# Preparation of a four-layer graph network on one core: adjacency casts issued earlier, the first head's scores by a product, x loaded by rows

## The chip, the cores and the metric

The kernel runs on one core of a Trainium2 chip, in one launch. The metric is the device time of an execution in microseconds (us). The kernel before took 2358.74 us (median of three runs, 2350.66 to 2361.85). The profile is one further execution of 2364.72 us, whose span from the first to the last instruction is 2363.0 us.

## The reference

Four layers in a row work on the same 4096 nodes with 64 features and a dense 4096 x 4096 adjacency of zeros and ones. Each is `x = x + layer(relu(layernorm(x)))`. The change lies in layer 0, a graph attention with eight heads of 32 features, six on the features and two whose scores come from given "intent" vectors:

```python
mask = (adj > 0)[None]
Wh_s = jnp.einsum('nf,hfo->hno', x, W_sp)
f1 = jnp.einsum('hno,ho->hn', Wh_s, a_sp[:, :NHID])
f2 = jnp.einsum('hno,ho->hn', Wh_s, a_sp[:, NHID:])
e_s = jax.nn.leaky_relu(f1[:, :, None] + f2[:, None, :], ALPHA)
h_s = jax.nn.elu(_masked_attend(e_s, mask, Wh_s))     # softmax over the neighbours, times Wh_s
... # two intent heads alike, their scores from intent_embeds
Who = h @ W_out
... # one more attention over Who, its scores from a_out
```

Layers 1 to 3 (a hyperbolic layer, a mean over neighbours, and one that weights the last 100 neighbours) are not touched.

## The kernel before, in words

The 4096 nodes are 32 blocks of 128 (`NB` = 32, `P` = 128). Since exp(leaky_relu(a + b)) is a product of two factors on each side of a + b = 0, a head's softmax sums need only the sign of a + b for each pair of nodes. For a head and a half of the receiving nodes (2048 of them, `HW`) the kernel does, for each pair of sender blocks `j0`:

- two signs `st`, 128 x 2048 each, from `srow` (the receivers' scores, the same row on all 128 partitions) and the senders' scores `nt`: on ScalarE, every fifth one on VectorE (`split_edges`, L1127 and L1132);
- `B`, the signs and the adjacency bits `mres`, and for most pairs `C`, the remaining edges (VectorE, L1136 and L1140);
- the sums `accB`, `accD`, `accC`, `accL` on TensorE (L1371), with the head's values `ybh` and `ych` as weights.

Such a head and half is called a unit here; there are sixteen, half 0 first. In unit 0 TensorE also forms `dm`, the sums that tell of receivers without edges, with `YD` as weights and the raw `mres` as data. At a unit's end ScalarE copies accB (L1506) and accC, VectorE accD and accL.

**The adjacency.** `mres` is eight buffers, each four sender blocks by 2048 receivers, one byte an entry. GpSimd's queue loads them from the float32 adjacency and casts on the way, 4 MB read for 1 MB written each. Four are issued in the preparation (L1160), the other four when `srow` of unit 0 has landed (`transfers_after`, L1090 to L1093, makes GpSimd read one element first). The other half of the receivers is cast later in the same manner, in the units of heads 1 to 4.

**The preparation.** Two 512 KB loads bring `x` with nodes `(b p)`: block b, partition p. SyncE's queue then loads `FT`'s intent rows, the weights `rh` (W_sp, W_int and four vectors of a_int) and `ab` (a_sp). GpSimd loads `rho` (W_out) and `abo` (a_out). `layernorm_relu` (L943 to L953) makes `h` in two halves; `feature_rows` transposes it (`tr`, L959) and copies it to `FT` (L960); `w2sq`, `Mh`, `Qh` scale the weights; `pa` makes the score columns; `pw` (L1010) the output's score columns in `rho`. Then TensorE forms `pst` (all scores by node and head 0's values `z0`, L1236) and `prs` (scores as rows, L1260). The rows go to memory (`srow_d`, L1269) and come back on all partitions (`srow`, L1328). Exponentials `wn`, `fz` and the splits `fd`, `YD`, `ybh`, `ych` follow (`value_steps`, L1185 to L1191, L1104 to L1113). `mean` and `meanq` are the values of receivers without edges.

The values of the other seven heads are formed inside unit 0, in eight groups k (L1453): four products `pwh`, two copies into parts of `h` and `x`, which are free by then, and a store to `Z_d`. Each unit of half 0 reads its next head's part back (`zt`).

A scheduler sets the order on each engine from the order in the source and from what an instruction depends on[...]. Pools give memory: a pool opened after another has closed takes its place, and its first users wait for the last users of what lay there before. The signs `st`, `B`, `C` of the units lie in the pool `hwork`, opened after the preparation's pools have closed:

```python
B, C = split_edges(
    work,                       # pool "hwork"
    srow,
    nt[:, j0 : j0 + 2, hd],
    edges,
```

Of the kernel before, what the change touches and what calls it, by code (L numbers as in the profile page):

```python
# [9 lines left out]
F32 = mybir.dt.float32  # L10
BF16 = mybir.dt.bfloat16
F16 = mybir.dt.float16
# [6 lines left out]
ALU = mybir.AluOpType  # L19
AX = mybir.AxisListType  # L20
# [4 lines left out]
P = 128  # L25
N = 4096
NB = N // P
D = 64
# [802 lines left out]
def kernel(  # L831
# [67 lines left out]

    def load_x():  # L900
        for bs in halves:
            nc.sync.dma_start(x[:, bs], x_in.rearrange("(b p) f -> p b f", p=P)[:, bs])

    load_x()
    h = npool.tile([P, NB, D], F32, name="h")

# [29 lines left out]

    def layernorm_relu():
        with tc.tile_pool(name="ln", bufs=1) as wide:
            for bs in halves:
                nb = bs.stop - bs.start  # L940
                hb = h[:, bs]
                mean = small("ln_mean", nb)
                nc.vector.tensor_reduce(mean, x[:, bs], AX.X, ALU.add)  # L943
                nc.vector.tensor_scalar(mean, mean, 1.0 / D, None, ALU.mult)
                nc.vector.tensor_tensor(hb, x[:, bs], over(mean, D), ALU.subtract)
                sq = wide.tile([P, nb, D], F32, name="ln_sq", tag="wide")
                nc.vector.tensor_tensor(sq, hb, hb, ALU.mult)
                var = small("ln_var", nb)
                nc.vector.tensor_reduce(var, sq, AX.X, ALU.add)
                nc.scalar.activation(var, var, AF.Sqrt, bias=eps_t, scale=1.0 / D)  # L950
                nc.vector.reciprocal(var, var)
                nc.vector.tensor_tensor(hb, hb, over(var, D), ALU.mult)
                nc.vector.tensor_scalar(hb, hb, 0.0, None, ALU.max)  # L953
# [43 lines left out]
    with ExitStack() as l0:  # L997
# [4 lines left out]
        rho = lp.tile([P, NC2, D + 2], F32, name="rho")  # L1002
        nc.gpsimd.dma_start(rho[:, :, 0:D], W_out.rearrange("(c p) o -> p c o", p=P))
        abo = lp.tile([P, 2, D], F32, name="abo")
        nc.gpsimd.dma_start(
            abo.rearrange("p s d -> p (s d)"), a_out.unsqueeze(0).to_broadcast([P, 2 * D])
        )
        for s in range(2):
            pw = spool.tile([P, NC2, D], F32, name="pw", tag="pw")
            nc.vector.tensor_tensor(  # L1010
                pw,
                rho[:, :, 0:D],
                abo[:, s : s + 1, :].to_broadcast([P, NC2, D]),
                ALU.mult,
            )
            nc.vector.tensor_reduce(rho[:, :, D + s], pw, AX.X, ALU.add)

        def feature_loads(hp):
# [15 lines left out]
            for i in range(HI):  # L1034
# [7 lines left out]
                a_sp.rearrange("h o -> (h o)").unsqueeze(0).to_broadcast([F, HS * 2 * O]),  # L1042
            )
            return FT, rh, ab

# [11 lines left out]

        def feature_rows(FT, ps):
            for g in range(NG):
                transpose_to(  # L1060
                    FT[0:F, g * G : (g + 1) * G],
                    [h[:, b, :] for b in range(g * GB, (g + 1) * GB)],
                    F,
                    ps,
                    nc.scalar.copy,
                )
# [14 lines left out]
        def edges_of(q, hf):  # L1081
            return adjT[q * JT * P : (q + 1) * JT * P, hf * HW : (hf + 1) * HW].rearrange(
                "(t p) i -> p t i", p=P
            )
# [10 lines left out]
        def first_half(q):  # L1095
            return mres[q].bitcast(F8), edges_of(q, 0)


# [3 lines left out]
        def split16(hi, lo, src, tmp):  # L1102

            nc.scalar.copy(hi, src)  # L1104
            nc.vector.tensor_tensor(tmp, src, hi, ALU.subtract)
            nc.scalar.activation(lo, tmp, AF.Copy, scale=LO)  # L1106
# [47 lines left out]
        YD = lp.tile([P, NB, 4, NH], BF16, name="YD")  # L1154
        nc.gpsimd.memset(YD, 0.0)
        Mh = lp.tile([P, NH], F32, name="Mh")
        meanq = lp.tile([P, NH, 2, O], F16, name="meanq")
        nc.gpsimd.memset(meanq, 0.0)
        for q in range(NQ // 2):
            nc.gpsimd.dma_start(*first_half(q))  # L1160
        srow_d = dram.tile([NH, N], F32, name="srow_d")
# [5 lines left out]
        Z_d = dram.tile([NB // 4, P, (NH - 1) * 4 * O], F32, name="Z_d")  # L1167
        vpool = ea.enter_context(tc.tile_pool(name="values", bufs=2))

        def value_tiles():  # L1170
# [28 lines left out]
        with ExitStack() as pa:  # L1199
# [28 lines left out]
            nc.vector.tensor_copy(rhz[0:F, 2 * NH :], rhq[:, 0:O])  # L1228
            layernorm_relu()
            feature_rows(FT, ps)  # L1230
            st16 = hp.tile([P, NB, 2 * NH], F32, name="st16")
            z0 = hp.tile([P, NB, O], F32, name="z0")
            for b0 in range(0, NB, 8):
# [14 lines left out]
            cm = col_maxs(tm, NH, "cmax")  # L1248
            
            cm = cm.unsqueeze(1).to_broadcast([P, NB, NH])  # L1250

            rs = hp.tile([K0, O], F32, name="rs")
            nc.vector.memset(rs, 0.0)
            nc.vector.tensor_copy(rs[:, 0:NH], rh[:, HO : HO + NH])
            sr = hp.tile([P, 2, G], F32, name="sr")
            for k in range(2):
# [38 lines left out]
            pss = ps.tile([P, HO], F32, name="pss", tag="misc")  # L1295
            nc.tensor.matmul(pss, lhsT=frep, rhs=rhq, start=True, stop=True)
            mean = work.tile([P, NH, O], F32, name="mean", bufs=1)
            nc.scalar.copy(mean, pss.rearrange("p (h o) -> p h o", o=O))
            mhl = work.tile([P, NH, 2, O], F16, name="mhl", bufs=1)
            split16(mhl[:, :, 0, :], mhl[:, :, 1, :], mean, mean)  # L1300
            for q in range(NS):
                nc.scalar.copy(meanq[q * O : q * O + 1], mhl[q * O : q * O + 1])
        with ExitStack() as ha:
# [4 lines left out]

            by_g = h.rearrange("p b d -> p (b d)").rearrange("p (s i) -> p s i", i=G)
            def load_products(zt, hd):  # L1310
                src = Z_d.rearrange("k p (h i) -> p k h i", h=NH - 1)[:, :, hd - 1, :]
                nc.sync.dma_start(zt.rearrange("p (k b) o -> p k (b o)", b=4), src)

            pending = None
            for hf in range(2):
# [9 lines left out]
                for hd in range(NH):  # L1325
                    first = hd == 0
                    srow = vpool.tile([P, HW], F32, name="srow", tag="srow")
                    nc.sync.dma_start(  # L1328
                        srow,
                        srow_d[hd : hd + 1, hf * HW : (hf + 1) * HW].to_broadcast([P, HW]),  # L1330
                    )
                    if hf == 0 and first:
                        transfers_after(srow[0:1, 0:1], *(first_half(q) for q in range(NQ // 2, NQ)))
                    yb, yc = now
# [46 lines left out]
                    for j0 in range(0, NB, 2):  # L1381
# [4 lines left out]
                        B, C = split_edges(  # L1386
                            work,
                            srow,
# [52 lines left out]
                        if hf == 0 and hd > 0 and j0 % (NB // 2) == 8 and later:  # L1441
                            transfers_after(B.bitcast(U8)[0:1, 0, 0:4], *later.pop(0))
                        if hf == 0 and first and j0 < NB // 2:

                            k = j0 // 2
                            Z = (h, x)[k // 2 % 2].rearrange("p b d -> p (b d)").rearrange(
                                "p (s i) -> p s i", s=2
                            )[:, k % 2, 0 : (NH - 1) * 4 * O]
                            for b in range(0, 4, 2):
                                pw = ps.tile([P, 2, NH - 1, O], F32, name="pwh", tag="misc")  # L1450
                                for i in range(2):
                                    c = (4 * k + b + i) * P
                                    nc.tensor.matmul(  # L1453
                                        pw[:, i].rearrange("p h o -> p (h o)"),
                                        lhsT=FT[0:F, c : c + P],
                                        rhs=rhq[:, O:],
                                        start=True,
                                        stop=True,
                                    )
                                (nc.vector.tensor_copy if b else nc.scalar.copy)(  # L1460
                                    Z.rearrange("p (h b o) -> p b h o", b=4, o=O)[:, b : b + 2], pw
                                )
                            nc.sync.dma_start(Z_d[k], Z)
                        if hf == 0 and first and j0 == NB // 2 + 2:
                            load_products(zt, hd + 1)
                        if j0 >= (NB // 2 + 6 if first else NB // 2 - 2):
                            next(coming, None)
# [1054 lines left out]
```

## Time and profile before

| | us |
|---|---|
| Median of three runs (lowest, highest) | 2358.74 (2350.66, 2361.85) |
| Profiled execution | 2364.72 |
| Its span | 2363.0 |
| TensorE busy over the span | 1990.4 (84%) |
| VectorE busy | 1842.6 (78%) |
| ScalarE busy | 1666.3 (71%) |
| GpSimd busy | 82.9 (4%) |
| First accB product of unit 0 | 77.44 |
| Copy of accB, units 0 and 1 | 148.74, 211.02 |

A row of the timeline names the start, the busy time, the engine, the line, the operation, output and inputs, and in brackets the idle time before it with what ended it. In the chain of waits each row is a stretch (start, length) of the work that ended last. "DMA" there is a transfer that was waited for, "issue" time in which the engine waited for nothing that the profile shows. The shares of busy time are means over four layers with different limits; the change is read from the first 150 us alone.

### The profile page before, as it was taken

What the parts mean: (1) busy time and instruction counts of PE and PEld (TensorE: products, weight loads), DVE (VectorE), ACT (ScalarE), POOL (GpSimd) and SP (SyncE); (2) the same over time, 40 slices, a digit from 0 to 9 for tenths busy, and PEclk for the clock granted to TensorE, in tenths of its full rate; (3) what the DMA queues carried; (4) which work ended last, traced back from release to release, by engine and by line L of the source; (5) the groups of instructions that cost most, each with busy time, mean ns of one, the idle gap of its engine ahead of it and who ended that gap; (6) DMA issues with size and microseconds to landing.
All of it is one profiled execution on the core that took longest, in us unless ns stands there. A gap on an engine that the chain in (4) does not pass through costs nothing.

```text
span 2363.0 us, 43206 instructions
## 1 busy us (share of the span) xinstructions
PE 1990.4 (84%) x18884; PEld 946.6 (40%) x18884; DVE 1842.6 (78%) x2180; ACT 1666.3 (71%) x1385; POOL 82.9 (4%) x123
## 2 busy tenths in 40 slices
PE   4788889889999999858996479999999951969997
PEld 2444444444444444424443233343343420444332
DVE  6588988887999899797666798888888979554452
ACT  4779999998899899554553488888888841113775
POOL 1000000000000000000000000000000000000000
PEclk7899999999999999879997789999999985965998
DMA  9944654243111120365441101110011103824993
GB/s 137 157 106 74 111 97 117 91 179 118 47 46 64 47 73 2 126 236 205 153 142 50 32 14 32 31 32 26 23 36 32 32 0 137 327 78 148 318 324 115
DMA packets 120206, 243.16 MB, mean 103 GB/s; under 512 B 14867, under 2 KB 87683, under 8 KB 103459
## 3 DMA queue, kind: packets, MB, share of 16 engines
q1 hardware_dynamic: 105126, 196.99, 23.9%
q0 software_dynamic: 14880, 43.31, 10.5%
q8 instruction: 150, 2.46, 0.4%
q14 instruction: 50, 0.41, 0.1%
HBM read 247.97 MB, written 51.03 MB: 127 GB/s over the span
## 4 chain that ended last, share of the span: by engine, by line
PE 38%; ACT 25%; DVE 20%; DMA 9%; issue 7%; POOL 0%; SPq 0%; DVEq 0%; ACTq 0%; POOLq 0%
ACT st L1132 14%; DMA raw<-in_adj_dram 5%; PE accB L1371 4%; DVE B L1136 3%; PE pu L2033 3%; ACT xt L1989 3%; PE nacc L2224 2%; ACT root L1989 2%; PE pl L2002 2%; ACT at L1989 2%; PE acco L1720 2%; PE acco L1718 2%; PE pl L2005 2%; PE acco L1719 2%; DVE at L2055 2%
## 5 line engine op out<-in xcount | busy, mean ns | idle before, releaser
L1132 ACT ACTIVATE st<-srow,nt 128x2048 int8<-128x2048 f32 x397 | 764.0, 1993 | 66.8 <-DVE B L1136 63.2
L1371 PE MATMUL accB<-B,ybh 128*32 128x512 fp8e4 x6144 | 485.1, 385 | 4.8 <-DVE B L1136 4.7
L1136 DVE TENSOR_TENSOR B<-st,mres 128x1024 int32<-128x1024 int32 x256 | 312.1, 1220 | 60.3 <-ACT st L1132 24.0
L1371 PEld LDWEIGHTS <-ybh 128*32 128x32 bf16 x8192 | 241.8, 98 | 258.5 <-issue 61.1
L1371 PE MATMUL accD<-B,ybh 128*32 128x512 fp8e4 x2048 | 285.9, 385 | 22.5 <-DVE h L1504 22.5
L1140 DVE TENSOR_TENSOR C<-B,mres 128x1024 int32<-128x1024 int32 x200 | 243.9, 1220 | 9.9 <-PE accL L1371 1.0
L1371 PE MATMUL accL<-C,ych 128*32 128x512 fp8e4 x1600 | 198.2, 382 | 25.2 <-DVE h L1507 25.2
L928 DVE SCALAR_TENSOR_TENSOR raw<-raw 128x2048 f32<-128x2048 f32 x64 | 146.3, 2288 | 87.0 <-DMA raw<-in_adj_dram 87.0
L1371 PE MATMUL accC<-C,ych 128*32 128x512 fp8e4 x1600 | 198.7, 384 | 7.3 <-DVE C L1140 7.3
L1371 PEld LDWEIGHTS <-ych 128*32 128x32 f16 x4096 | 141.1, 97 | 147.8 <-issue 47.1
L1989 ACT ACTIVATE sg<-pl,rb 128x512 f32<-128x512 f32 x256 | 163.1, 684 | 50.9 <-PE pl L2005 47.6
L1132 ACT ACTIVATE st<-srowo,nto 128x1024 int8<-128x1024 f32 x108 | 118.7, 1141 | 81.2 <-DVE B L1136 79.3
L2415 ACT ACTIVATE w3b<-pv 128x1024 int16<-128x1024 f32 x128 | 131.0, 1023 | 51.9 <-PE pv L2406 51.4
L2033 PE MATMUL pu<-XAf,LDf 66*128 66x512 f32 x288 | 150.5, 626 | 13.7 <-DVE at L2040 12.5
L1127 DVE TENSOR_SCALAR st<-srow,nt 128x2048 uint8<-128x2048 f32 x115 | 147.8, 1285 | 0.8
L2070 PE MATMUL acci<-sg,VQ 128*65 128x512 f32 x288 | 137.6, 602 | 4.8 <-DVE sg L2068 4.6
L2224 PE MATMUL nacc<-m,HH 128*128 128x512 fp8e4 x256 | 61.8, 390 | 74.6 <-ACT HH L2213 74.6
L2040 DVE TENSOR_SCALAR at<-pu 128x512 f32<-128x512 f32 x144 | 95.1, 684 | 25.9 <-PE pu L2033 25.8
L1718 PE MATMUL acco<-B,YBo 128*128 128x512 fp8e4 x256 | 98.2, 385 | 16.4 <-ACT YCo L1106 15.9
L2002 PE MATMUL pl<-nm,noid 128*128 128x512 fp8e4 x256 | 100.0, 391 | 12.2 <-ACT sg L1989 12.1
L2089 PE MATMUL accj<-sg,VQ 128*65 128x512 f32 x224 | 107.6, 596 | 0.4 <-DVE sg L2088 0.4
L1720 PE MATMUL acco<-C,YCo 128*128 128x512 fp8e4 x256 | 96.1, 385 | 4.3 <-DVE C L1140 3.4
(480 smaller groups left out, 3294.6 us busy)
## 6 DMA issues: line engine op xcount, KB each, us to landing
raw<-in_adj_dram SPq DMA_DIRECT2D x64, 1024.0 KB, 7.3
srow<-srow_d SPq DMA_DIRECT2D x16, 1024.0 KB, 7.2
mo<-edges SPq DMA_DIRECT2D x32, 512.0 KB, 5.3
noedge<-nmo POOLq DMA_DIRECT2D x32, 512.0 KB, 4.1
nm<-noedge SPq DMA_DIRECT2D x64, 256.0 KB, 2.9
m<-edges SPq DMA_DIRECT2D x16, 1024.0 KB, 7.0
m<-edges SPq DMA_DIRECT2D x32, 512.0 KB, 6.3
mres<-in_adj_dram POOLq DMA_DIRECT2D x8, 1024.0 KB, 30.3
```

The lines of the kernel that those rows point to most:

```text
L928: nc.vector.scalar_tensor_tensor(raw, raw, 0.0, raw, ALU.is_gt, ALU.not_equal, accum_out=bad[:, c : c + 1])
L1127: nc.vector.tensor_scalar(st[:, i, :].bitcast(U8), srow, negs[:, i : i + 1], EDGE, ALU.is_gt, ALU.mult)
L1132: nc.scalar.activation(st[:, i, :], srow, AF.Sign, bias=negs[:, i : i + 1], scale=-1.0)
L1136: nc.vector.tensor_tensor(B.bitcast(I32), st.bitcast(I32), edges.bitcast(I32), ALU.bitwise_and)
L1140: nc.vector.tensor_tensor(C.bitcast(I32), B.bitcast(I32), edges.bitcast(I32), ALU.bitwise_xor)
L1371: nc.tensor.matmul(acc[k * O : (k + 1) * O, :], lhsT=values, rhs=moving(k), start=start, stop=stop,)
L1718: nc.tensor.matmul(acc1[k], lhsT=YB[:, j, 0:P], rhs=B[:, ks], **fl)
L1720: nc.tensor.matmul(accC[k], lhsT=YC[:, j].rearrange("p s d -> p (s d)"), rhs=C[:, ks], start=(j == 0), stop=False,)
L1989: tc.keep_in_program_order(nc.scalar.activation(*args, **kw))
L2002: nc.tensor.matmul(pl, lhsT=noid, rhs=nm[:, b, :].bitcast(F8), start=True, stop=False)
L2033: nc.tensor.matmul(pu, lhsT=LD[:, j * P : (j + 1) * P], rhs=XA[:, grp(gi)], start=True, stop=True,)
L2070: nc.tensor.matmul(accs[gi], lhsT=XQ[:, gj * GB + b, :], rhs=w[:, b, :], start=(gj == 0 and b == 0), stop=(gi == gj and b == GB - 1),)
```

## The change

- `x` is loaded with nodes `(p b)`: partition p holds 32 successive nodes, so each half is 128 rows of 4 KB. The copies to `FT` put the columns back in the order of nodes. (The later load of x for the residual keeps `(b p)`.)
- The first four casts stand earlier in GpSimd's queue. The other four wait for `cmax`, the largest scores, instead of `srow`.
- `rho` and `abo` are loaded by SyncE, at the end of `feature_loads`; `out_weights` (the `pw` steps) stands after `feature_rows`.
- `srow` of unit 0 is made by four products of 128 x 512 (`psr`), with head 0's score column repeated 128 times (`srep`) as weights, and four copies out of PSUM; the rows still go to memory for the other units.
- `z0` and `sr` lie in `x`. `meanq` is written for all partitions, with zeros from a factor `rows`, instead of by four copies of one row.
- `st`, `B`, `C` get a pool of their own (`signs`), opened before the preparation; the first layernorm's squares use its `C`.
- Groups 0 and 1 of the other heads' products stand ahead of unit 0, and each later group two pairs of blocks sooner; the first `zt` load comes two pairs sooner, and the value steps of head 1 one pair.

In the built program VectorE's queue has, around the end of the layernorm: `w2sq`, the first half's last two steps, `pa`, `rhz`, the second half's product, the first `pw`, `Qh`, the second half's ReLU. On TensorE six `pwh` and four `psr` products stand between `pst` and `prs`, and 49 of the 128 `dm` products ahead of the first accB product, where before it was 70. On ScalarE the copies of `sr` stand between the first exponential and the other two, and the first two signs between the casts of head 0's values.

```diff
-    def load_x():
+    def load_x(form="(b p) f -> p b f"):
         for bs in halves:
-            nc.sync.dma_start(x[:, bs], x_in.rearrange("(b p) f -> p b f", p=P)[:, bs])
-
-    load_x()
+            nc.sync.dma_start(x[:, bs], x_in.rearrange(form, p=P)[:, bs])
+    load_x("(p b) f -> p b f")
...
-    def layernorm_relu():
-        with tc.tile_pool(name="ln", bufs=1) as wide:
+    def layernorm_relu(pool=None, tag="wide"):
+        with ExitStack() as ln:
+            wide = pool or ln.enter_context(tc.tile_pool(name="ln", bufs=1))
...
-        nc.gpsimd.dma_start(rho[:, :, 0:D], W_out.rearrange("(c p) o -> p c o", p=P))
         abo = lp.tile([P, 2, D], F32, name="abo")
-        nc.gpsimd.dma_start(
-            abo.rearrange("p s d -> p (s d)"), a_out.unsqueeze(0).to_broadcast([P, 2 * D])
-        )
-        for s in range(2):
...
+        def out_loads():
+            nc.sync.dma_start(rho[:, :, 0:D], W_out.rearrange("(c p) o -> p c o", p=P))
+            nc.sync.dma_start(
+                abo.rearrange("p s d -> p (s d)"), a_out.unsqueeze(0).to_broadcast([P, 2 * D])
+            )
+
+        def out_weights():
+            for s in range(2):
+                pw = spool.tile([P, NC2, D], F32, name="pw", tag="pw")
+                nc.vector.tensor_tensor(
+                    pw, rho[:, :, 0:D], abo[:, s : s + 1, :].to_broadcast([P, NC2, D]), ALU.mult,
+                )
+                nc.vector.tensor_reduce(rho[:, :, D + s], pw, AX.X, ALU.add)
...
+            out_loads()
             return FT, rh, ab
...
         def feature_rows(FT, ps):
+            by_p = FT[0:F].rearrange("f (p b) -> f p b", b=NB)
             for g in range(NG):
                 transpose_to(
-                    FT[0:F, g * G : (g + 1) * G],
+                    by_p[:, :, g * GB : (g + 1) * GB],
                     [h[:, b, :] for b in range(g * GB, (g + 1) * GB)],
                     F,
                     ps,
-                    nc.scalar.copy,
+                    lambda dst, t: nc.scalar.copy(dst, t.rearrange("f (b p) -> f p b", p=P)),
                 )
...
+        for q in range(NQ // 2):
+            nc.gpsimd.dma_start(*first_half(q))
...
         nc.gpsimd.memset(YD, 0.0)
-        nc.gpsimd.memset(meanq, 0.0)
-        for q in range(NQ // 2):
-            nc.gpsimd.dma_start(*first_half(q))
...
+        epool = ea.enter_context(tc.tile_pool(name="signs", bufs=2))
...
-            layernorm_relu()
+            layernorm_relu(epool, "C")
             feature_rows(FT, ps)
+            out_weights()
-            z0 = hp.tile([P, NB, O], F32, name="z0")
+            z0 = x_flat[:, 2 * G :].rearrange("p (b o) -> p b o", o=O)
...
+            transfers_after(cm[0:1, 0:1], *(first_half(q) for q in range(NQ // 2, NQ)))
+            srep = hp.tile([K0, P], F32, name="srep")
+            nc.vector.tensor_copy(srep, rh[:, HO : HO + 1].to_broadcast([K0, P]))
+            srow0 = vpool.tile([P, HW], F32, name="srow", tag="srow")
+            for g in range(HW // G):
+                pr = ps.tile([P, G], F32, name="psr", tag="misc")
+                nc.tensor.matmul(
+                    pr, lhsT=srep, rhs=FT[:, g * G : (g + 1) * G], start=True, stop=True
+                )
+                (nc.vector.tensor_copy if g % 2 else nc.scalar.copy)(srow0[:, g * G : (g + 1) * G], pr)
-            sr = hp.tile([P, 2, G], F32, name="sr")
+            sr = x_flat[:, 0 : 2 * G].rearrange("p (k i) -> p k i", k=2)
...
-            nc.scalar.copy(mean, pss.rearrange("p (h o) -> p h o", o=O))
-            mhl = work.tile([P, NH, 2, O], F16, name="mhl", bufs=1)
-            split16(mhl[:, :, 0, :], mhl[:, :, 1, :], mean, mean)
-            for q in range(NS):
-                nc.scalar.copy(meanq[q * O : q * O + 1], mhl[q * O : q * O + 1])
+            nc.vector.tensor_scalar(
+                mean, pss.rearrange("p (h o) -> p h o", o=O), rows, None, ALU.mult
+            )
+            split16(meanq[:, :, 0, :], meanq[:, :, 1, :], mean, mean)
...
+            for k in range(2):
+                other_products(k)
...
-                    srow = vpool.tile([P, HW], F32, name="srow", tag="srow")
-                    nc.sync.dma_start(
-                        srow,
-                        srow_d[hd : hd + 1, hf * HW : (hf + 1) * HW].to_broadcast([P, HW]),
-                    )
-                    if hf == 0 and first:
-                        transfers_after(srow[0:1, 0:1], *(first_half(q) for q in range(NQ // 2, NQ)))
+                    srow = srow0
+                    if hf or hd:
...
                         B, C = split_edges(
-                            work,
+                            epool,
...
-                        if hf == 0 and first and j0 < NB // 2:
-                            k = j0 // 2
...
+                        if hf == 0 and first and j0 // 2 + 2 < NB // 4:
+                            other_products(j0 // 2 + 2)
-                        if hf == 0 and first and j0 == NB // 2 + 2:
+                        if hf == 0 and first and j0 == NB // 2 - 2:
                             load_products(zt, hd + 1)
-                        if j0 >= (NB // 2 + 6 if first else NB // 2 - 2):
+                        if j0 >= (NB // 2 + 4 if first else NB // 2 - 2):
                             next(coming, None)
```

## The prediction

> **What bounds the kernel now.** Nothing in the change lies beyond the preparation and the first of 16 units (half 0, head 0), so I read the chain of waits from 0 to 250 us, then ScalarE's timeline over unit 0, then the DMA queues by window. The chain (start, us, what):
>
> ```profile
> 10.51 3.31 DMA abo<-in_L_gnn_a_out_dram
> 13.92 0.49 DVE pw L1010 x2
> ...
> 23.58 0.59 DVE h L953
> 24.34 2.42 PE tr L959 x16
> 26.76 8.42 PE pst L1236 x64
> 35.18 3.62 PE prs L1260 x16
> ...
> 41.77 6.22 DMA srow_d<-sr
> 48.14 8.98 DMA srow<-srow_d
> 57.31 19.64 DMA mres<-in_adj_dram
> 76.99 1.04 PE dm L1371 x6
> ```
>
> The layernorm sets the path to 24 us, the features and scores to 39, the round trip of the scores through memory to 57, and the fifth adjacency cast to 77, where TensorE first adds. ScalarE's timeline (start, busy, what):
>
> ```profile
> 57.88 7.68 ACT L1132 ACTIVATE st<-srow,nt 128x2048 int8<-128x2048 f32 x4
> ...
> 82.20 3.90 ACT L1132 ACTIVATE st<-srow,nt 128x2048 int8<-128x2048 f32 x2 [6.50 <-DVE B L1136]
> ...
> 148.74 0.56 ACT L1506 COPY h<-accB 128x512 f32<-128x512 f32 x1
> ```
>
> The signs start at 57.88; unit 0 ends with the copy of accB at 148.74. The next unit's copy comes at 211.02: 62.3 us, ScalarE busy for most of it. So what moves 148.74 moves the end; all later work shifts with it.
>
> The DMA answers over 51 to 57, 8.4 to 11 and 14 to 26 us (queue: packets, MB, share of 16 engines):
>
> ```profile
> q0 software_dynamic: 170, 0.33, 54.8%
> q1 hardware_dynamic: 165, 1.22, 50.0%
> ...
> q1 hardware_dynamic: 833, 0.18, 39.2%
> ...
> q0 software_dynamic: 600, 1.20, 105.1%
> ```
>
> While both queues have work they send equal numbers of packets, whatever their size (170 to 165). SP's weights (W_sp to ab) are 833 packets, sent in 2.6 us with no cast beside them. Casts alone fill all 16 engines: 600 packets in 12 us, 0.32 us each on its engine, so one cast (512 packets) takes 10.2 us.
>
> **What the Trainium skill says.** "DMA: Bandwidth & Descriptors", section "Queues, rings and completion order": an engine goes round-robin between the queues at packet granularity, with 9 to 17 descriptors typical in a packet. The trace agrees on the turns (170 to 165); whether SP's 128 to 512-byte rows go one or many to a turn beside a cast, no view of before shows. That is the main unknown. "TensorE: Matmul & The Clock Gate", Part 1: the clock is halved until some 3.4 us of sustained work. The trace agrees: clock 0.50 from 38 to 50 and 70 to 80 us, 1.00 from 80; two pwh products took 1.86 us at 62.5 and 1.02 at 85. "SBUF — State Buffer", section "Door 1: The DMA port swizzle": SBUF has 16-byte lines, PSUM 8-byte ones, and crossing to a new line costs. The strided casts of fd (256 elements, 1.04 us against 0.39 for a plain cast) agree.
>
> **The change, part by part.**
>
> *Casts sooner.* The first cast takes rho's place on POOL (1.39 us, was 12.62); three follow ident (10.5), the last four follow cmax rather than srow's landing at 57. In exchange rho and abo go to the end of SP's queue, and all of SP's weights now run beside casts. One packet to a turn: 833 packets plus 416 for rho and abo (256 + 128 rows and 2x16 completions) are 1,249, over 16 engines 78 turns of 0.32 + 0.02 us = 26.6 us. x and FT's 32 long packets go first, to about 8 us. So W_int lands near 20, ab near 26, abo near 34.6 us. SP's issues go on without harm; nothing waits behind them before 40 us.
>
> *VectorE's queue.* x by 4 KB rows (256 packets for 4,096) lets it start at about 3.8 instead of 5.22 us, and ident and abo no longer stop it at 10.6 and 13.9. But w2sq (needs W_int) now stands before the first half's last steps, pa (ab) after them, and the first pw (rho, abo) before the second half's ReLU. Its own work reaches w2sq at 14.4, so it stalls to 20, at pa to 26, at pw to 35. After pw: 0.25 + 0.19 + 0.68 us, the ReLU ends at 35.9, was 24.18. That takes the whole gain of x and 11.7 us more. Behind it stand the transposes, pst, and all else.
>
> *FT by node.* The eight copies become strided in PSUM and SBUF. Before, the last ended 3.3 us after the ReLU. Bounds for the four on the path: 0 (width alone counts) to +5 us (fd's excess, about 2.5 ns an element, on 512 elements). I take +2: FT is whole at 41.2, was 27.5. The copies scatter, so pst starts only now: 8.6 us, to 49.8.
>
> *Products ahead, scores by product.* Between pst and prs come six pwh products and four psr (128x512 out). Full clock: three pwh pairs at 0.95 and four psr at 1.05 (two passes of pu's row, 150.5/288 = 0.52) and prs 2: 9.1 us. Half clock: 5.6 + 8.4 + 3.6 = 17.6. I take 12, to 61.8. ScalarE's queue holds the sr copies ahead of the second exponential, so copy 0.6, wn 0.45, fz 0.4: the exponentials end at 63.3, was 42.84.
>
> *From there to the signs.* VectorE needs about 13 us for the value steps as before (42.6 to 55.8). The store and reload of srow (39.4 to 57.2) is gone, the meanq copies (2.5 us) are two casts, and with their own memory the signs can go between the casts. Added up along both queues, the first two signs are done 14 us after the exponentials and the third starts at +15.1: 78.4, where before it was at 61.7. The first accB product is then at about 78.7, was 77.44.
>
> *Unit 0.* Casts go on from 4 us and four have landed by about 52, the fifth near 66, ahead of their use: TensorE's waits for mres (4.2 + 9.4 us) go, and with them ScalarE's 6.5. From the third sign: 30 signs at 1.92 = 57.6, five pwh copies 2.6, four value casts 4.1, and 6 us of waits (from 107 to 149 ScalarE waited 6.4 for B): 70.3, so accB's copy is at 148.7, was 148.74. TensorE has two pwh pairs fewer left at its start (1.9 us) against 21 more dm products (1.1); I leave both in that wait. **Sum: 0.0 us.** The profiled execution took 2364.72 us (span 2363.0 and 1.7 around it), 6 above the median 2358.74, so I predict 2358.7.
>
> At nothing: small(), rows, srep (0.1 to 0.3 us each, under VectorE's stalls or fsum's 4.4 us before pst); 4 KB reading of x alone; earlier zt loads (before, they were waited for 1.9 + 1.6 us, in the 6 above). If abo came early, x's gain would count again (below).
>
> **Rivals.** *B, rows share turns.* If several small rows pass per turn, each of the ten loads waits two or three turns and abo is there by some 15 us, before pw's place at 21.5. The ReLU ends at 22.5, 13.4 us sooner than above, and so does all behind it: accB's copy at 135.3, time 2345.3. For it: the skill's packets; against: 170 to 165 over packets of 8 and 2 KB, one to one. *C, slower.* abo's landing sets the ReLU from 21.5 us on, microsecond for microsecond. If a row costs two cast packets instead of one, or its completion has to wait as well, 78 turns cost 0.66 us, abo lands at 60 and the time is 2384; from a landing past 46 us it is over 0.5% slower. For it: the scores' small stores took 6.2 us to land beside casts at 41.8; against: 54.8% and 50.0% shares, an even split. *D, it doesn't do what it says:* three of the first four casts wait for ident and the other four for a cmax that moves from 36.7 to about 51; that brings the casts some 10 us forward, and none of it is on the path once the signs start at 78. That is inside the forecast.
>
> **How the numbers follow.** One row to a turn (forecast) 0.60, with some 7 us either way from the clock (3 down, 5.6 up), the strided copies (2 down, 3 up) and the waits of unit 0 (3 down, 4 up). B 0.27, 13.4 faster with 6 around it. C 0.13. About 0.5% (11.8 us) is what a measurement of this kernel can tell from no change: the three runs of before spread over 0.47%. Faster by more: 0.03 of the forecast's share, 0.16 of B's: 0.19. Slower: 0.03 and 0.12: 0.15. The rest, 0.66, within. The range goes from B's lower part, 2339, to the near part of C, 2374; the forecast's own is 2350 to 2367.
>
> **What would show it.** Right: VectorE waits for rho or abo (DMA) at pw some 8 us and before that for the weights at w2sq and pa; ReLU's end near 36; transposes after it; first accB near 79; no wait of dm for mres over 2 us; the copy of accB within 7 us of 148.7; units 1 to 15 unchanged at about 62 us. Wrong: abo landed by 20 us (then B), or pw held past 46 (then C), or a wait in unit 0 that takes back the 13.6 us of mres elsewhere.

## The result, and the profile after

The changed kernel takes 2371.80 us (median of 20 runs, 2353.42 to 2379.30), the kernel before, run beside it, 2357.38 us (20 runs, 2344.86 to 2365.51). The ratio is 1.0059, 95% interval 1.0039 to 1.0079: slower by 0.59%, some 14 us, just over the 0.5% that the prediction named as its bound. It forecast no change (2358.7, range 2339 to 2374). Executions of one kernel differ by some 20 us, and the work after the last of the sixteen units, which the change leaves as it was, took from 1369.6 to 1387.4 us in the traces of the runs below.

The chain of waits of the changed kernel from 0 to 156 us (start, us, what) answers to the first one shown of before:

```profile
2.20 15.18 DMA rh<-in_L_gnn_W_sp_dram
17.40 16.41 DMA abo<-in_L_gnn_a_out_dram
35.01 3.60 PE tr L961 x16
39.27 13.89 PE pst L1248 x64
53.16 4.78 PE pwh L1343 x12
57.94 6.96 PE psr L1269 x8
64.89 1.90 PE prs L1282 x16
...
80.61 3.53 PE dm L1418 x29
...
85.19 0.76 PE accB L1418 x12
...
140.04 7.16 DMA zt<-Z_d
```

Before, the layernorm led to 24 us and the scores' round trip to 57. Now two small weight loads lead to 34 us: abo (0.06 MB) is 16.41 us under way. pst is on the path with 13.89 us (8.42 before). The round trip and the waits for mres are gone, and still the first accB product comes at 85.12 (77.44 before; both from the timeline, whose rows start a little sooner than the chain's). VectorE's waits from 0 to 70 us (total, times, longest) say who held its queue:

```profile
DVE pw L1016 <- DMA abo<-in_L_gnn_a_out_dram: 5.7, 1, 5.7
...
DVE w2sq L1218 <- DMA rh<-in_L_gnn_W_int_dram: 3.9, 1, 3.9
...
DVE pa L1057 <- DMA ab<-in_L_gnn_a_sp_dram: 3.2, 1, 3.2
```

The DMA queues from 14 to 33 us (packets, MB, share of 16 engines) say why the weights are late:

```profile
q0 software_dynamic: 968, 1.92, 99.8%
q1 hardware_dynamic: 944, 0.26, 8.6%
```

q0 is the casts, q1 the weights: 968 to 944 packets, so the two queues sent equal numbers, a small row for each 2 KB of a cast. ScalarE's timeline (start, busy, what, idle time before and its releaser):

```profile
81.53 11.47 ACT L1143 ACTIVATE st<-srow,nt 128x2048 int8<-128x2048 f32 x6
...
149.62 5.79 ACT L1143 ACTIVATE st<-srow,nt 128x2048 int8<-128x2048 f32 x3 [4.34 <-DVE B L1147]
155.31 0.56 ACT L1534 COPY h<-accB 128x512 f32<-128x512 f32 x1
```

Unit 0 ends at 155.31 instead of 148.74 (+6.6). Unit 1's copy comes at 219.20 (210.92 before; the 211.02 of the table above is from the chain), the copy of unit 8 at 629.44 (620.04, +9.4), that of the last unit at 988.55 (978.92, +9.6). The span ends 5.8 later, for the work after the last unit took 1380.3 us against 1384.1. The profiled execution of before (2364.72) was 7.3 us over the median of its 20 runs, that of after (2370.60) 1.2 under its own: 5.9 + 7.3 + 1.2 is the 14.4 between the medians. So the traces show 9.6 us of it, all in layer 0.

### The profile page after: what moved, and what is told of

It reads as the page before. It is cut to its first block, busy times and chain, and to the rows that moved or that the text cites. A ratio compares the mean times of both kernels' runs of the same rounds, so it can differ in the third digit from the quotient of the medians.

```text
span 2368.8 us, 43218 instructions
## 1 busy us (share of the span) xinstructions
PE 2000.6 (84%) x18892; PEld 952.4 (40%) x18892; DVE 1844.3 (78%) x2185; ACT 1664.1 (70%) x1382; POOL 79.8 (3%) x120
## 4 chain that ended last, share of the span: by engine, by line
PE 41%; ACT 26%; DVE 19%; issue 7%; DMA 6%; SPq 0%; POOL 0%; DVEq 0%; ACTq 0%; POOLq 0%
ACT st L1143 15%; DVE B L1147 4%; PE pu L2061 3%; PE accB L1418 3%; ACT xt L2017 3%; PE nacc L2252 2%; ACT root L2017 2%; PE pl L2030 2%; PE acco L1748 2%; PE acco L1746 2%; ACT at L2017 2%; PE pv L2434 2%; PE acco L1747 2%; PE pl L2033 2%; DMA raw<-in_adj_dram 2%
## 5 line engine op out<-in xcount | busy, mean ns | idle before, releaser
L1418 PE MATMUL accC<-C,ych 128*32 128x512 fp8e4 x1600 | 198.6, 384 | 13.1 <-DVE C L1151 13.1
L2033 PE MATMUL pl<-MOV,one 128*128 128x512 bf16 x256 | 99.8, 390 | 0.0
```

Source lines behind the costliest of these rows:

```text
L1418: nc.tensor.matmul(acc[k * O : (k + 1) * O, :], lhsT=values, rhs=moving(k), start=start, stop=stop,)
L2033: nc.tensor.matmul(pl, lhsT=one3, rhs=MOV[:, grp(tgt)], start=False, stop=True,)
```

## The experiments

**Theory A:** with a cast queued first, each small row of SP's weights waits for a cast packet; VectorE's queue stops for them, and everything behind pays, TensorE's clock included. **Rival B:** the products put ahead of unit 0 cost the time. **Rival C:** unit 0 itself, or its transfers. The ratio is to the kernel before, run on the same chip; "accB" is the copy that ends unit 0 (one profiled execution).

| run | starts from | ratio, 95% interval | pst, us | accB, us |
|---|---|---|---|---|
| before | | 1 | 8.42 | 148.74 |
| after | | 1.0059 (1.0039 to 1.0079) | 13.89 | 155.31 |
| e1_weights_late | after | 1.0007 (0.998 to 1.0035) | 11.84 | 146.15 |
| e2_casts_behind_abo | after | 1.0021 (1.0 to 1.0042) | 10.81 | 148.06 |
| e3_before_casts_sooner | before | 1.0079 (1.0048 to 1.0109) | 13.86 | 167.82 |
| e4_before_scores_product | before | 1.0153 (1.0108 to 1.0197) | 10.53 | 183.80 |
| e5_products_in_unit | after | 1.0041 (1.002 to 1.0061) | 11.95 | 152.42 |
| e6_before_scores_product_2 | before | 1.006 (1.0037 to 1.0083) | 8.65 | 162.10 |
| e7_before_casts_and_rows | before | 1.0042 (1.0021 to 1.0062) | 13.89 | 158.87 |
| e8_two_queues | e1 | 0.9973 (0.9953 to 0.9993) | 10.12 | 144.06 |
| e9_warm | after | 1.0034 (1.0019 to 1.005) | 11.84 | 149.24 |
| e10_two_queues_2 | e1 | 1.0012 (0.9986 to 1.0038) | 10.17 | 147.84 |
| e11_two_queues_products | e10 | 0.9975 (0.9957 to 0.9993) | 10.54 | 140.34 |

### e1: the output weights later

```diff
             feature_rows(FT, ps)
-            out_weights()
...
+            done = nc.vector.tensor_scalar(
                 mean, pss.rearrange("p (h o) -> p h o", o=O), rows, None, ALU.mult
             )
             split16(meanq[:, :, 0, :], meanq[:, :, 1, :], mean, mean)
+            with tc.issue_after(done.ins):
+                out_weights()
```

> The changed kernel with one edit: the output layer's weights (pw and its sums, 4 VectorE instructions) are ordered after the last value step of the preparation, so that no VectorE step ahead of the scores waits for abo; the loads and casts stay where they are. Theory A (SP's small weights, one row to a turn beside casts, hold VectorE's queue, and what stands behind it pays): pw's wait of 5.7 us goes, the second half's ReLU ends near 28.8 instead of 34.9 us (only the waits for W_int at 20 and ab at 25.5 stay), the copy of accB of unit 0 comes 6 us sooner (149) or, if TensorE then finds a faster clock for pst (13.9 us, 8.6 before), up to 11 sooner (144): median 2361 to 2366, 6 to 11 under the changed kernel. Rival B (the products between pst and prs, and their place in ScalarE's order, cost the time): pst and all behind it start sooner but the copy of accB moves by less than 2 us, median 2369 to 2373. Rival C (something in unit 0 or 1 itself): the first signs come 6 us sooner and the copy of accB doesn't follow.

The chain of e1:

```profile
7.66 17.90 DMA ab<-in_L_gnn_a_sp_dram
29.29 2.75 PE tr L961 x12
33.24 11.84 PE pst L1247 x64
```

ab leads to 25.56 now, and the wait for abo has left the path. pst starts 6.0 us sooner, as theory A forecast, and takes 2.05 less; accB is 9.2 us sooner. The 6.0 us are the wait's; that the shorter pst follows from it isn't shown, since pst is as short in e5 (11.95) with the wait in place. The ratio falls by 0.52% (12 us), and its interval no longer meets that of the changed kernel. Four VectorE instructions at the wrong place in a queue were most of the loss.

### e2: the first casts behind abo

```diff
-        for q in range(NQ // 2):
-            nc.gpsimd.dma_start(*first_half(q))
...
             FT, rh, ab = feature_loads(hp)
+            transfers_after(abo[0:1, 0, 0:1], *(first_half(q) for q in range(NQ // 2)))
             features(rh, ab)
```

> The changed kernel with one edit: the first four casts are issued after a one-element copy of abo on GpSimd, so they start when SP's weights are all in. Theory A: W_int, ab and abo land by about 10 us, no wait at w2sq, pa, pw; the second half's ReLU ends near 22.5 (34.9 in the changed kernel), pst starts near 27 and, its clock as before, takes 8.6 instead of 13.9; casts run from about 10.5 instead of 1.4 and are still ahead of their use. The copy of accB comes 12 to 18 us sooner: 137 to 143; median 2354 to 2360. Rival B (products ahead of unit 0): 3 us sooner at most, 2368 or more. Rival C (the later casts are missed: mres waits of dm return): the signs start 12 us sooner, and 5 us or more of it is lost to waits for mres.

The weights' waits are gone, the second ReLU ends at 22.7 and pst starts at 25.52, as forecast. The end isn't: accB is at 148.06, not 137 to 143. ScalarE's timeline of e2:

```profile
48.01 2.00 ACT L1141 ACTIVATE st<-srow,nt 128x2048 int8<-128x2048 f32 x1 [1.06 <-DVE srow L1271]
...
54.80 0.51 ACT L1300 ACTIVATE fz<-st,consts 128x256 f32<-128x256 f32 x1
...
117.40 1.05 ACT L1199 CAST ybh<-pz 128x1024 bf16<-128x1024 f32 x1 [6.88 <-DVE pz L1194]
...
148.06 0.56 ACT L1533 COPY h<-accB 128x512 f32<-128x512 f32 x1
```

The first sign starts 26 us sooner than in the changed kernel and the unit ends 7 us sooner. The trace shows three things that took part of the difference; how much each took isn't shown. The first two signs stand ahead of the exponentials in the built order of ScalarE, so these start only at 54.80. From 70 to 102 us TensorE is busy for 31.57 of 32 us. And the chain has two transfers late in the unit:

```profile
102.68 8.42 DMA Z_d<-x
111.29 4.83 DMA zt<-Z_d
```

The casts, begun near 16 us, fill the engines to about 112, and the last store of Z shares them; zt can be read only after it. VectorE waits for zt for 10.1 us in this unit (4.3 in the changed kernel). Theory A holds for the preparation, but the time that it forecast (2354 to 2360) was missed: 2365.37. Rival C was right that a part of the gain is lost, and wrong about the cause: the trace has no wait for mres.

### e3 and e7: the casts sooner, on the kernel before

e3 issues the first four casts at the start of GpSimd's queue and rho and abo at the end of SP's, as the change does; e7 adds x by rows.

```diff
-        nc.gpsimd.dma_start(rho[:, :, 0:D], W_out.rearrange("(c p) o -> p c o", p=P))
...
+            out_loads()
             return FT, rh, ab
...
+        for q in range(NQ // 2):
+            nc.gpsimd.dma_start(*first_half(q))
...
+            out_weights()
# e7 alone:
+    load_x("(p b) f -> p b f")
...
+                    by_p[:, :, g * GB : (g + 1) * GB],
```

> The kernel before with one part of the change: the first four casts issued at the start of GpSimd's queue, rho and abo at the end of SP's, pw after the transposes in the program as in the changed kernel; nothing else. Theory A: the weights land at 20, 26 and 34 us as in the changed kernel, ReLU ends near 35 instead of 24.2, pst takes 12 to 14 instead of 8.4, srow lands near 70 to 74 instead of 57; some of it is given back since mres is waited for less (13.6 us before): the copy of accB 5 to 12 us later than before's 148.7, median 2362 to 2369. Rival B (the products ahead cost it): within 2 us of before, 2356 to 2359. Rival C (casts sooner gain by themselves, since mres's waits go): 2350 or less.

> The kernel before with two parts of the change: casts sooner with rho and abo on SP (as e3_before_casts_sooner), and x by 4 KB rows with the strided copies into FT. Theory A: x lands near 5 instead of 21 us as in e3, since 256 packets instead of 4,096 take turns with the casts; the weights as in the changed kernel (20, 26, 34), pst 12 to 14 us long, the exponentials end near 58, the signs start near 74 and the copy of accB comes near 155 to 160: about 10 us under e3 and 8 above before, ratio to before 1.002 to 1.006. Rival B (x by rows does nothing here, the delay of e3 is the weights alone): as e3, ratio 1.007 to 1.010.

e3 is slower than I forecast (accB at 167.82, not 154 to 161), for a reason that I had left out. VectorE's wait in e3:

```profile
DVE ln_mean L943 <- DMA x<-in_x_dram: 15.9, 2, 12.4
```

x in its old form is 4,096 packets of 256 bytes, and they too have to share with the casts: from 5 to 10 us SP's queue sent 162 packets to 210 of the casts, and x lands at 21.4 us. e7 gives x 256 packets and the wait falls to 3.7, accB to 158.87, as its theory A forecast; pst is 13.89 as in the changed kernel. So x by 4 KB rows is what makes early casts bearable; what it is worth without them wasn't tried. e7's ratio, 1.0042, cannot be told from that of the whole change: the loss is there with these two parts alone, and the rest of the change (scores by product, own memory, products ahead) doesn't mend it.

### e4 and e6: the scores by product, on the kernel before

```diff
+            srep = hp.tile([K0, P], F32, name="srep")
...
+                nc.tensor.matmul(
+                    pr, lhsT=srep, rhs=FT[:, g * G : (g + 1) * G], start=True, stop=True
...
-                    srow = vpool.tile([P, HW], F32, name="srow", tag="srow")
+                    srow = srow0
+                    if hf or hd:
```

> The kernel before with one part of the change: the first head's scores are put on all partitions by four products, and the second four casts follow that row (they followed srow's landing); nothing else. Theory A: the row is there near 42 instead of 57 us, the signs start near 51 to 54 (held by the value steps and by the memory that they share with the preparation), the fifth cast lands near 67 instead of 77, so the copy of accB comes 4 to 9 us sooner: median 2348 to 2353. Rival B: four products at half the clock and their copies take back what the round trip gives: 2356 to 2360.

> The kernel before with the first head's scores by four products, and the second four casts after that row; it differs from e4_before_scores_product in that each cast is issued once (e4 issued the second four casts twice). Theory A: the row is there near 42 instead of 57 us, the casts go on without a gap, the fifth lands near 67 to 72 instead of 77, signs start near 58 to 62 (held by the value steps and the shared memory): the copy of accB 3 to 9 us sooner than 148.7, ratio 0.996 to 0.999. Rival B: the four products at half the clock take it back, ratio 0.999 to 1.002.

e4 issued the second four casts twice, so it says nothing of the scores by product: accB at 183.80. e6 issues each cast once, and both theories missed: 0.60% slower. The row is complete near 43 us, the casts run without a gap, and accB is 13 us later. TensorE's timeline of e6:

```profile
72.79 0.59 PE L1383 MATMUL dm<-mres,YD 128*32 128x512 fp8e4 x1 [10.23 <-DMA mres<-in_adj_dram]
...
83.56 1.90 PE L1383 MATMUL dm<-mres,YD 128*32 128x512 fp8e4 x16 [6.57 <-DMA mres<-in_adj_dram]
93.32 1.01 PE L1383 MATMUL dm<-mres,YD 128*32 128x512 fp8e4 x5 [7.87 <-DMA mres<-in_adj_dram]
93.76 1.85 PE L1383 MATMUL accB<-B,ybh 128*32 128x512 fp8e4 x12
```

The built order put 101 dm products ahead of the first accB. Each cast serves 16 of the 128, so these ask for the seventh cast; before it was 70 (the fifth), in the changed kernel 49 (the fourth). TensorE took them in that order: the first B was ready at 65.9 us, and the first accB came at 93.76. Casts land one after the other, here some 10 us apart, and the first accB stands behind the last one that its queue asks for. An order built for sooner transfers made the same transfers later on the path.

### e5: no products ahead of unit 0

```diff
-            for k in range(2):
-                other_products(k)
...
-                        if hf == 0 and first and j0 // 2 + 2 < NB // 4:
-                            other_products(j0 // 2 + 2)
+                        if hf == 0 and first and j0 // 2 < NB // 4:
+                            other_products(j0 // 2)
```

> The changed kernel with one part undone: no head's other products ahead of unit 0, they all stand in unit 0 as before (and the load of zt and the value steps two and two places later, as before). Theory A (the weights' wait behind casts is the loss): six pwh products (4.8 us) and two copies on ScalarE leave the stretch between pst and the exponentials, which end near 62.5 instead of 68.1, but unit 0 then carries two more pairs and gets zt later, so the copy of accB stays within 3 us of 155.3, median 2368 to 2374. Rival B (the products ahead are the loss): the copy of accB comes 5 us or more sooner, median 2366 or less.

The exponentials end 8.7 us sooner (59.5; 1.9 of it is a shorter pst), the zt waits in unit 0 grow to 9.5, and accB is 2.9 us sooner. That is theory A by a hair; rival B isn't most of the loss. The intervals of e5 and of the changed kernel overlap widely.

### e8, e10, e11: the weights in two queues

```diff
# e8, on e1: W_int, a_int and ab; e10, on e1: W_sp and ab
-            nc.sync.dma_start(
+            nc.scalar.dma_start(
# e10 and e11
+            summed = layernorm_relu(epool, "C")
+            with tc.issue_after(summed.ins):
+                features(rh, ab)
...
# e11: other_products as in e5
```

> e1_weights_late with one more edit: W_int, the four a_int columns and ab are issued from ScalarE's queue instead of SP's, so the small rows take their turns in two queues beside the casts. Theory A (each queue gets one turn per cast packet): ab lands within about 6 us, W_int near 12, W_sp near 17; VectorE waits at w2sq to about 17 and no more at pa, the second half's ReLU ends near 24 (28 in e1), pst starts 4 to 5 us sooner; the copy of accB of unit 0 near 141 to 146 (146.2 in e1), the rest being held by the transfers of Z and zt: ratio to before 0.996 to 1.000. Rival (the turns are shared by the software queue and all hardware queues together): ab and W_int land as in e1, at 20 to 26 us, and the time is that of e1.

e8 is faster than before (0.9973, interval under 1). The chain begins:

```profile
0.82 5.93 DMA ab<-in_L_gnn_a_sp_dram
7.23 14.16 DMA rh<-in_L_gnn_W_sp_dram
```

Theory A is right about the turns: from 14 to 15 us the casts sent 49 packets, SP's queue 48 and ScalarE's 48. That ab lands at 6.75 instead of 25.56 has a second reason: in the built order it is the first load of ScalarE's queue, where in e1 it stood behind W_sp, W_int and a_int. W_sp, left on SP, was issued only at 7.23 and landed at 21.4, not 17, so pa waited 7.1 us for it instead, and the second ReLU ends at 29.0 (29.1 in e1). pst starts 0.6 us sooner and takes 1.7 less. The forecast of accB and of the ratio held, by another way than the one forecast: of the 2.1 us that accB gains on e1, 1.7 are pst's, and the two ratios' intervals overlap.

> e1_weights_late with ab and W_sp (instead of none) issued from ScalarE's queue, and the weights' VectorE work (pa, w2sq, rhz and what lies between) ordered behind the layernorm's second sum of squares. Theory A: ab and W_sp land near 13 us, W_int near 15, before VectorE comes to them, so VectorE runs from x's landing to the second ReLU without a wait (ends near 20 to 22; 24 to 28 in e8 and e1), pst starts near 24 to 26. If the preparation's length still sets the end of unit 0, the copy of accB comes near 137 to 141 (144.1 in e8): ratio to before 0.994 to 0.996. Rival (with the weights out of the way the transfers bound unit 0: the eight casts, then the stores of Z and the load of zt): the copy of accB stays between 142 and 147 and the ratio at 0.996 to 0.999, as in e2 where the signs started at 48 us and accB ended at 148.

In e10 VectorE waits for no weight, the second ReLU ends at 20.3; pst starts at 28.60 since the transposes stand behind pmh, which needs w2sq. accB comes at 147.84, past both forecasts, and the chain says why:

```profile
41.38 33.50 DMA mres<-in_adj_dram
74.92 1.01 PE dm L1421 x5
...
76.98 1.40 PE accB L1421 x11
```

The signs start at 58.95, but the built order has 85 dm products ahead of the first accB, which ask for the sixth cast, and TensorE waits 7.3 us for it. It is e6's fault again.

> e10_two_queues_2 with the other heads' products all in unit 0, as before the change (none ahead of it). Theory A (the products ahead of unit 0 cost as much ahead as they save within it): the exponentials end some 6 us sooner, the copy of accB within 3 us of e10's, ratio within 0.002 of e10's. Rival B (they cost on the path ahead of the exponentials): the copy of accB 4 us or more sooner than e10's. Rival C (zt late): the copy of accB 4 us or more later than e10's, with waits for zt of over 8 us in unit 0.

e11 has 46 dm products ahead of the first accB and no wait for mres; accB comes at 140.34, the earliest here, 7.5 us before e10. By the number that is rival B, but the order changed too, so it isn't shown that the products' place did it, and the ratios' intervals of e10 and e11 just overlap. VectorE's waits to 141 us show what is left:

```profile
DVE pz L1197 <- DMA zt<-Z_d: 9.6, 2, 6.2
```

e8 and e11 (0.9973 and 0.9975) are the versions that beat both kernels. Their traces agree: the last unit's copy comes at 974.74 and 971.59, where before it came at 978.92.

### e9: TensorE kept busy

```diff
+                if g == NG // 2:
+                    warm = ps.tile([P, G], F32, name="warm", tag="misc")
+                    for k in range(3):
+                        nc.tensor.matmul(
+                            warm[0:D], lhsT=h[:, 0, :], rhs=..., start=True, stop=True
+                        )
```

> The changed kernel with one addition: three 512-column fp32 products of h into a PSUM tile that nobody reads, on TensorE between the transposes of the first and of the second half, where it waits for VectorE (28 to 35 us). Theory 1 (TensorE's idle stretch before the second transposes cost it the clock): pst takes 8.4 to 11 instead of 13.9 us, and the copy of accB comes 3 to 5 us sooner: median 2366 to 2369, ratio to before 1.003 to 1.005. Theory 2 (the clock falls for a reason that short work doesn't change; in the kernel before it fell at 32 us in the middle of pst): pst stays at 12 to 14 us, the added products may push the transposes back by up to 2 us, ratio 1.005 to 1.008.

TensorE's timeline of e9:

```profile
27.64 4.25 PE L1071 MATMUL warm<-h 128*64 128x512 f32 x6
34.62 3.28 PE L961 MATMUL tr<-ident,h 128*64 128x128 f32 x16 [2.73 <-DVE Qh L1232]
38.57 11.84 PE L1254 MATMUL pst<-rhz,FT 96*128 96x48 f32 x64 [0.67 <-ACT FT L1079]
```

pst is 2.05 us shorter, accB 6.1 us sooner, the ratio 1.0034 within the forecast of theory 1; pst itself lies between the two theories' ranges. But this does not show that the added products did it. TensorE's timeline of e5, which has no such products:

```profile
34.88 3.19 PE L961 MATMUL tr<-ident,h 128*64 128x128 f32 x16 [6.90 <-DVE Qh L1226]
38.77 11.95 PE L1248 MATMUL pst<-rhz,FT 96*128 96x48 f32 x64 [0.70 <-ACT FT L1073]
```

There TensorE stood idle for 6.90 us ahead of the transposes, as in the changed kernel, and pst was as short as in e9; in e7 it stood idle for 6.91 and pst took 13.89. So pst differs by 2 us at one and the same idle stretch. e9's built order differs too: 85 dm products stand ahead of the first accB, where the changed kernel has 49. And the intervals of e9 and the changed kernel overlap (1.0039 to 1.0050). What the added products are worth stays open.

## Why the prediction was wrong, step by step

- *What sets the path* was right: one row to a turn (968 to 944). W_int was there by 19.96, ab by 25.5, abo by 33.8, forecast 20, 26, 34.6; the second ReLU ended at 34.87, forecast 35.9. The waits for mres (13.6 us before) went as forecast. Rival "rows share turns" fell.
- *The strided copies of FT* were put at +2; they took 0.58 us each, as before. From the ReLU to the whole FT took 4.35 us, forecast 5.3, so FT was whole at 39.22, forecast 41.2: with the earlier ReLU 2.0 us to the good.
- *"The copies scatter, so pst starts only now: 8.6 us"* is the step that failed: pst took 13.89. The term was taken from a row of before in which TensorE had just worked with no gap over 0.62 us; here it stood idle from 28 to 35 us. 5.3 us.
- *Products ahead, scores by product*, 12 us between bounds of 9.1 and 17.6: 13.6, 1.6 more.
- *From the exponentials to the third sign* 15.1: 13.4, 1.7 less, and 0.2 less just ahead of it.
- *Unit 0* from the third sign, 70.3: 73.8, 3.5 more. ScalarE's longest wait (4.34 at 149.62) is behind a second load of zt (7.16 us). The 6 us of waits had been carried over from before.
- Sum: -2.0 + 5.3 + 1.6 - 0.2 - 1.7 + 3.5 = +6.5; measured +6.6 at accB.
- *"Units 1 to 15 unchanged"* was off as well: they took 3.1 us more (+9.6 at the last unit's copy). Unit 1 took 63.9 us, 62.2 before, VectorE waiting 4.4 us for zt.

So the mechanism was right: what leads to the ReLU, and which waits go. The step mis-sized was pst, put at 8.6 us and measured at 13.89, with unit 0's waits and the later units after it. The prediction gave bounds for the products behind pst ("3 down, 5.6 up" is their 9.1 to 17.6 around 12), but none for pst, though the clock and an idle stretch of TensorE both follow from what it says elsewhere. That the smaller terms took 2.3 us of the 8.8 back is luck. So is it that 2371.80 lies within the range: its upper part was kept for a later landing of abo (C), and abo landed as forecast. The time is 13.1 us over the 2358.7 that was forecast; the traces place 9.6 of it, and the rest is less than the spread of the work after the last unit.

Why pst was slow is open. In the kernel before its records went at about 10 in a microsecond from 28 to 32 us and at about half that from 33 us, and the profile's granted clock fell from 1.00 to 0.50 between. In the changed kernel they went at 4.6 in a microsecond all through (64 in 13.89 us), so half speed fits; but there the profile's granted clock reads 1.00 from 20 to 68 us. The half speed is thus read from the pace, and the idle stretch alone doesn't set it (e5 and e7 above).

The Trainium skill, "TensorE: Matmul & The Clock Gate", Part 1, has the clock doubled after some 3.4 us of sustained work. Here pst doesn't show that: in the kernel before it slowed down at 32 us in the middle of such work, and in the changed kernel TensorE worked from 35.01 us with gaps under 1 us, and pst and the pwh after it still ran slowly; only prs, at 64.89, ran fast (1.90 us; 3.62 before), 30 us on. The measurement decides; what sets the moment is open. On "DMA: Bandwidth & Descriptors", section "Queues, rings and completion order", the turns by packet agree; its 9 to 17 descriptors to a packet do not show for these small rows, which go one to a turn: in the one microsecond of e8 named above, 16 engines sent 48 of SP's to 49 of the casts.

Not settled: why unit 1 waits longer for zt. In its trace the stores of `ybh` (1 MB), of `ych` (0.5 MB) and the load of zt are issued at 175.5, 180.7 and 181.2 us and zt takes 8.0; before they are issued at 162.0, 177.2 and 177.6 and zt takes 5.9. That fits transfers that share the engines, and no run tests it. Nor is it settled where the profiled execution of before lost its 7 us against the median, or what the signs' own memory is worth by itself, which wasn't tried.

## What to carry to other kernels

Before a large transfer is issued sooner, count the small packets that will be on the other queue beside it: each waits for one large packet on its DMA engine (0.32 us here, 16 engines side by side). VectorE's queue then passes the last landing on to all that stands behind it: the second ReLU of the changed kernel, which needs nothing of abo, started 0.4 us after abo had landed (33.8). Put work that needs a late load behind work that doesn't, as e1 did with four instructions. And when one part of a schedule moves, read the built order again on every engine: in e6 accB came 13 us later than before, and in e10 TensorE waited 7.3 us, where products that wait for later casts had moved ahead of the ones that were ready.

## What the runs showed of the hardware that I had not expected

- Two hardware queues beside a cast queue each get turns: 49 packets of the casts, 48 of SP's queue and 48 of ScalarE's from 14 to 15 us (e8).
- The same 64 pst records took 8.42 to 13.89 us. With the same idle stretch of 6.9 us ahead of the transposes they took 11.95 in e5 and 13.89 in e7.
- The granted clock that the profile shows and the pace of the records can differ: in the changed kernel it reads 1.00 while pst goes at 4.6 records in a microsecond; in e5 the same records go at about that pace where it reads 0.50 (42 to 48 us).
- Reading PSUM by 512-byte strides and writing SBUF in 16-byte runs cost nothing on ScalarE: 0.58 us for 64x512 in either form.
- x by 256-byte packets beside a cast was whole at 21.4 us (e3); by 4 KB packets the second half was read at 7.89 (e7).
